# A four-layer AdaLN/FFN kernel: another order for layer 0's folded attention, filler transposes on TensorE, zeros in pieces, a bias split moved to another engine

## The chip, the cores and the metric

The kernel runs on one core of a Trainium2 chip, as one launch. The metric is the device time of one execution in microseconds; lower is better. The core has five engines that run their own instruction streams: PE (TensorE: matmuls and transposes), DVE (VectorE), ACT (ScalarE), POOL (GpSimd) and SP (SyncE, here only an issuer of transfers). Transfers (DMA) are issued by SP, ACT or POOL from their own streams and run on 16 DMA engines.

## The reference

Tokens are x of shape (32, 64, 256): 2048 tokens of 256 features in 32 sequences, and one condition vector of 256 features per sequence. All values are float32. Four layers follow one another; each is `x = x + ffn(cond(x))`, with a part that conditions the tokens and a feed-forward part:

- Layer 0: attention with 16 heads of every token against two keys, a learnt no-op key and a key made from the condition of its sequence, then a projection; then a router (softmax over 8 experts, the best two are chosen), experts of 256 to 1024 to 256 with a GELU and room for 320 tokens each, and the weighted sum of their outputs, which is added to x.
- Layer 1: a shared expert and experts that are chosen per sequence from the pooled tokens, then a mixture with entmax weights.
- Layer 2: a recurrence over the 64 positions of a sequence, with three terms of a bias, then experts again.
- Layer 3: attention and feed-forward parts with norms, and a gated feed-forward whose weights are rounded to four-bit floats.

For layer 0's attention, with two keys, the softmax of a head is a function of one difference of scores:

```python
score = q . (k_cond - k_noop)                  # per token and head
w     = exp(min(score, 0)) / (exp(min(score,0)) + exp(-max(score,0)))
out   = v_noop + w * (v_cond - v_noop)         # per head, then W_proj and b_proj
```

## The kernel before

The 2048 tokens lie as 16 tiles of 128 tokens (`NT`), in four groups of four tiles (`NG`, `GT`). PE's products go to banks of PSUM (`bank`, 512 columns; `wide`, 1024 columns). `evacuate` copies a bank to SBUF by ACT and DVE in turn: one counter, `self.turn`, decides for every call in the whole program, so that a copy that no longer goes through it changes the engine of all later ones. The instructions of each engine stand in the order in which a scheduler puts them by their priority in the program; `issue_after(mark)` places an instruction right behind another one on its engine.

*Layer 0's attention* (`fold_scores`, `fold_output`, `layer0`). Instead of making q for each token, the kernel folds Wq into the keys. PE turns `cond` (L179); DVE copies it to `condT` and ACT makes `siluT` from the same bank (L182; used in layer 1 only). PE multiplies it with `wkv` (L769); DVE subtracts the no-op key (`diff`, L772) and spreads the difference over heads (`kx` for keys, `vx` for values, L775). PE turns the four leaves of Wq, a bank of 128 by 512, which is copied to `wqT` (L110 or L112, through `evacuate`). From `kx` and `wqT` PE makes `A` (L791, 8 matmuls). The constants of the scores, bq times the keys, are `z0`: 16 recorded matmuls of one column each (L797) and one copy (L800). After that come the values' half (L769 again) and a loop over the four groups: turn X (L138, the copies to `XT` all by ACT, L141), scores `XT` times `A` (L880), and the softmax of two (DVE L885, L886, L889 to L892; ACT L887, L888). `fold_output` turns W_proj (copied to `wpT` through `evacuate`), folds the router's weights in (L830 to L840) and makes `M` (L848). A last loop makes the features that go to the experts and the router scores, `C` (L905 to L907), the softmax of the router, and the flags of the two chosen experts (L915), and SP writes `C` to a table in DRAM.

The X loads, 512 KB each, are issued by ACT (L869), as are `wq` and `wkv`, and 2176 KB of zeros for `acc_c` (L923), a buffer in DRAM into which layer 1 adds its results. All other loads of the start are SP's, in program order.

*Layer 0's experts* (`routed`, `slots`, `positions`). PE counts each expert's tokens from the flags (L318, L319); DVE computes every token's slot. For each expert a pass of 16 matmuls (L405) turns one-hot matrices made by DVE (`oh`, L363) into the lists of tokens `l0f_read` and `l0f_add`. Four passes come before the first gather; the others, 64 matmuls, lie between the two matrices of expert 0 (the "half pass" ends the first lot). POOL gathers an expert's tokens from the table with indirect transfers (L490), PE turns them (L498), then come the first matrix (L448), GELU on ACT (L450), the second matrix (L457), the bias on DVE (L514), scaling on ACT (L515) and an indirect transfer by POOL that adds the rows to `acc` in DRAM (L516). These additions run one after the other. Beside the experts DVE rounds layer 3's weights (`last_weights`). After the last expert SP reads `acc` back as X (L931).

*Layer 1 and 2.* Layer 1 turns X (L138), writes it to a table (`table_x`, issued by ACT, L946), runs the shared expert and, from sums over the tokens (`agg`, L973 to L977, and `C`, L960), the choice of experts. In the same stretch `recurrent_weights` prepares layer 2: it splits the recurrence's bias `b` into three bfloat16 terms (cast L1120, copy L1121, subtraction L1123, on DVE). Layer 2 uses `slots` and `routed` with `by_position=True`.

*Fillers.* `repeat(mark, n)` issues n transposes of a constant matrix into a bank that nobody reads, right behind `mark` on PE (L118). Before the change only layer 2 has them, 14 after the counts, 3 after each of the first four slot passes and 4 after the half pass:

```python
if by_position:
    self.repeat(self.last_count, 14)
```

Of the kernel before, what the change touches and what calls it, by code (L numbers as in the profile page):

```python
# [9 lines left out]
F32 = mybir.dt.float32  # L10
# [4 lines left out]
AF = mybir.ActivationFunctionType  # L15
ALU = mybir.AluOpType
# [4 lines left out]
P = 128  # L21
NB = 32
NS = 64
N = NB * NS
NT = N // P
D = 256
DC = D // P
FF = 1024
FC = FF // P
NE = 8  # L30
# [3 lines left out]
NG = NT // GT  # L34
# [36 lines left out]
class Kernel:  # L71
# [53 lines left out]

    def transposed(self, out, srcs):

        ps = self.bank()
        for i, s in enumerate(srcs):
            self.nc.tensor.transpose(ps[:, i * P:(i + 1) * P], s, self.ident)  # L130
        self.evacuate(out, ps[:, :len(srcs) * P].rearrange("p (n q) -> p n q", q=P))

# [24 lines left out]
    def constants(self):  # L157
        nc, cp, I = self.nc, self.cp, self.I
        self.ident = cp.tile([P, P], F32, name="ident")
        make_identity(nc, self.ident)  # L160
        self.ones_row = cp.tile([1, 512], F32, name="ones_row")
        nc.gpsimd.memset(self.ones_row, 1.0)
        iota = cp.tile([P, P], I32, name="iota_i")
        nc.gpsimd.iota(iota, pattern=[[1, P]], base=0, channel_multiplier=0)
        self.iota = cp.tile([P, P], F32, name="iota")
        nc.vector.tensor_copy(self.iota, iota)
        part = cp.tile([P, 1], I32, name="part_i")
        nc.gpsimd.iota(part, pattern=[[0, 1]], base=0, channel_multiplier=1)
        self.part = cp.tile([P, 1], F32, name="part")
        nc.vector.tensor_copy(self.part, part)  # L170


        cond = self.xp.tile([NB, D], F32, name="cond")
        nc.sync.dma_start(cond, I["cond_1024"])
        self.condT = cp.tile([P, DC, NB], F32, name="condT")
        self.siluT = cp.tile([P, DC, NB], F32, name="siluT")
        ps = self.bank()
        for c in range(DC):
            nc.tensor.transpose(ps[:, c * NB:(c + 1) * NB], cond[:, c * P:(c + 1) * P], self.ident[:NB, :NB])  # L179
        view = ps[:, :DC * NB].rearrange("p (c b) -> p c b", b=NB)  # L180
        nc.vector.tensor_copy(self.condT, view)
        nc.scalar.activation(self.siluT, view, AF.Silu)  # L182

# [183 lines left out]
    def slots(self, pool, flags, capacity, name, indices, by_position=False):  # L367
# [3 lines left out]
        nc = self.nc  # L371
# [3 lines left out]
        pos = self.positions(pool, flags, NE, "sl")  # L375
        if by_position:
            self.repeat(self.last_count, 14)
        other = pool.tile(full, F32, name="sl_other")
# [15 lines left out]
        for e0, e1 in ((0, 1), (1, NE // 2), (NE // 2, NE)):  # L394
# [6 lines left out]
            for e in range(e0, e1):  # L401
                oh = self.one_hot(ohs, e, part)
                at = (e - e0) * nchunk
                for t in range(NT):
                    self.slot_pass = nc.tensor.matmul(ps[:, at:at + nchunk], oh[:, :, t], give[:, e, t],  # L405
                                                      start=(t == 0), stop=(t == NT - 1)).ins
                if by_position and e < 4:
                    self.repeat(self.slot_pass, 3)
# [52 lines left out]
    def routed(self, table, acc, pool, flags, capacity, w1s, b1, w2s, b2s, name, by_position=False, pieces=None,  # L461
               mark=None):

# [7 lines left out]
        with tc.tile_pool(name=f"{name}_h", bufs=2) as hp, tc.tile_pool(name=f"{name}_g", bufs=2) as gp:  # L471
            chunks = [(c, min(P, capacity - c * P)) for c in range(nchunk)]

            def fetch(e):
# [6 lines left out]
                if e == 0:  # L481
                    next(slots)
                    self.half_pass, self.half_oh = self.slot_pass, self.slot_oh
                    if by_position:
                        self.repeat(self.half_pass, 4)
                elif e == 1:
                    next(slots)
# [18 lines left out]
            for e in range(NE):  # L506
                w1, w2, b2, xeT, rows_of = coming
                h = self.hidden(hp, xeT[:, :, :capacity], w1, b1[:, e * FC:(e + 1) * FC], AF.Gelu, capacity)
                for c, rows in chunks:
# [4 lines left out]
                    nc.vector.tensor_tensor(y[:rows], ps[:rows, :D], b2[:rows], ALU.add)  # L514
                    nc.scalar.activation(y[:rows], y[:rows], AF.Copy, scale=rows_of[c][:rows, D + e:D + e + 1])  # L515
                    nc.gpsimd.indirect_dma_start(  # L516
# [225 lines left out]
    def fold_scores(self, kp, loads):  # L742
# [17 lines left out]
        nc.vector.tensor_tensor(less, cols[:, 0:4], cols[:, 4:8], ALU.subtract)  # L760
        bq = cols[:, 8:10]
        diff = kp.tile([P, 4, NB], F32, name="diff")
        by_head = []
        for i, name in enumerate("kv"):
# [14 lines left out]
            if i:  # L779
                break  # L780
            wqT = kp.tile([P, DC, D], F32, name="wqT")
            self.transposed(wqT.rearrange("p m (c q) -> p (m c) q", q=P),
                            [wq[:, c, m * P:(m + 1) * P] for m in range(DC) for c in range(DC)])
            self.A = kp.tile([P, DC, NB * NH], F32, name="A")
            half = NH // DC
            for c in range(DC):
# [6 lines left out]
                self.evacuate(self.A[:, c], ps)  # L793
            ps = self.bank()
            for g in range(NG):
                for m in range(DC):
                    nc.tensor.matmul(ps[:, g:g + 1], self.of_group(x, m, g), bq[:, m:m + 1],  # L797
                                     start=(m == 0), stop=(m == DC - 1))
            self.z0 = kp.tile([P, NG], F32, name="z0")
            nc.vector.tensor_copy(self.z0, ps[:, :NG])  # L800

# [12 lines left out]
    def of_group(self, x, m, g):  # L814

        return x[:, m, g * 2 * GT:(g + 1) * 2 * GT].rearrange("p b h -> p (b h)")

    def fold_output(self, kp, loads, vx):
# [32 lines left out]
    def layer0(self):  # L851
# [11 lines left out]
        with tc.tile_pool(name="l0s", bufs=1) as sp:  # L863
            with tc.tile_pool(name="l0c", bufs=1) as kp, tc.tile_pool(name="l0t", bufs=2) as tp:
# [7 lines left out]
                for g in range(NG):  # L872
                    for t in range(g * GT, (g + 1) * GT, 2):
                        self.tile_features(XT, self.X, t, nc.scalar.copy)

                    ps = self.bank()
# [7 lines left out]
                    w = kp.tile([P, P], F32, name=f"at_w{g}")  # L884
                    nc.vector.tensor_scalar(mx, ps[:, :P], self.z0[:, g:g + 1], 0.0, ALU.add, ALU.max)  # L885
                    nc.vector.scalar_tensor_tensor(d, ps[:, :P], self.z0[:, g:g + 1], mx, ALU.add, ALU.subtract)  # L886
                    nc.scalar.activation(w, d, AF.Exp)  # L887
# [30 lines left out]
                nc.sync.dma_start(acc_rows[:, NT], self.X[:, 0])  # L918

            self.accc = self.dp.tile([N + P, D], F32, name="acc_c")  # L920
            zero = self.xp.tile([P, D], F32, name="zero")
            nc.gpsimd.memset(zero, 0.0)
            nc.scalar.dma_start(self.accc.rearrange("(t p) d -> p t d", p=P),  # L923
                                zero.unsqueeze(1).to_broadcast([P, NT + 1, D]))
            with tc.tile_pool(name="fp4w", bufs=1) as kp:
                pieces = self.last_weights(kp)
                self.routed(table, acc, sp, flags, capacity, I["L0_ffn_w1"], self.bias["L0_ffn_b1"],
                            I["L0_ffn_w2"], I["L0_ffn_b2"], "l0f", pieces=pieces)
        self.X = self.rp.tile([P, NT, D], F32, name="X", tag="X")
# [169 lines left out]
    def recurrent_weights(self, rp):  # L1099
# [19 lines left out]
        for i in range(3):  # L1119
            nc.vector.tensor_copy(cut, b)  # L1120
            nc.vector.tensor_copy(three[i * NB:i * NB + 1], cut[i * NB:i * NB + 1])  # L1121
            if i < 2:
                nc.vector.tensor_tensor(b, b, cut, ALU.subtract)  # L1123
        ones = rp.tile([K, NB], BF16, name="b_ones")
# [901 lines left out]
```

## Time and profile before

| | |
|---|---|
| median of 3 runs | 1856.86 us (1856.2, 1856.86, 1864.89) |
| the profiled execution | 1859.04 us, its span 1857.3 us |
| granted TensorE clock, mean | 0.886 |
| busy: PE, DVE, ACT, POOL | 1573.2, 711.3, 597.5, 574.3 us |
| layer 0's attention to the first slot pass | 0 to 64.08 us |
| layer 0's experts | 64 to 253.7 us |
| layer 1 from the first turn of X | 259.31 us on |

The profile follows one execution. Times are in us from the start of the span; a row of the timeline gives the start, the duration, the engine, the source line, the operation with its output and inputs, the number of instructions in the group, and in brackets how long the engine had been idle and whose work ended that. PEld is PE's load of weights, which runs beside PE. A row with the letter q behind the engine (ACTq, SPq) is the issuing of a transfer, not the transfer. The granted clock is the share of full speed that the TensorE had. A window's row gives the busy time of each engine with the number of instructions, then the clock, the busy share of the DMA engines and GB/s.

### The profile page before, as it was taken

What the parts mean: (1) busy time and instruction counts of PE and PEld (TensorE: products, weight loads), DVE (VectorE), ACT (ScalarE), POOL (GpSimd) and SP (SyncE); (2) the same over time, 40 slices, a digit from 0 to 9 for tenths busy, and PEclk for the clock granted to TensorE, in tenths of its full rate; (3) what the DMA queues carried; (4) which work ended last, traced back from release to release, by engine and by line L of the source; (5) the groups of instructions that cost most, each with busy time, mean ns of one, the idle gap of its engine ahead of it and who ended that gap; (6) DMA issues with size and microseconds to landing.
All of it is one profiled execution on the core that took longest, in us unless ns stands there. A gap on an engine that the chain in (4) does not pass through costs nothing.

```text
span 1857.3 us, 27210 instructions
## 1 busy us (share of the span) xinstructions
PE 1573.2 (85%) x10195; PEld 1216.6 (66%) x10195; DVE 711.3 (38%) x2402; ACT 597.5 (32%) x1308; POOL 574.3 (31%) x740
## 2 busy tenths in 40 slices
PE   6799997999996939999798899999655768778767
PEld 5567766888886728888676576667443546546445
DVE  3684034111111171111224510100556578786765
ACT  2222332333331203333211123222235444655443
POOL 0234311233320013332100333422235445555452
PEclk9689998999997959999888899999766779787789
DMA  7455552466632055665214154432301100101000
GB/s 267 138 148 137 133 139 67 144 203 185 201 95 88 6 162 158 202 190 160 65 29 113 37 140 120 124 94 61 95 30 35 35 18 24 35 12 32 15 12 12
DMA packets 158408, 183.84 MB, mean 99 GB/s; under 512 B 37540, under 2 KB 137536, under 8 KB 158272
## 3 DMA queue, kind: packets, MB, share of 16 engines
q1 hardware_dynamic: 123920, 143.34, 24.1%
q0 software_dynamic: 21248, 29.24, 8.9%
q10 hardware_dynamic: 13104, 9.47, 1.7%
q8 instruction: 83, 1.36, 0.3%
q14 instruction: 53, 0.43, 0.1%
HBM read 152.22 MB, written 29.79 MB: 98 GB/s over the span
## 4 chain that ended last, share of the span: by engine, by line
PE 28%; DVE 9%; POOL 6%; issue 5%; ACT 4%; DMA 2%; SPq 0%; POOLq 0%; DVEq 0%; ACTq 0%
PE bank L457 6%; PE bank L448 6%; PE bank L1172 3%; PE bank L1921 2%; PE bank L1805 2%; PE bank L1728 1%; PE bank L1502 1%; PE bank L1863 1%; DMA acc<-y,pl_add 1%; PE bank L1938 1%; ACT squares L1647 1%; PE wide L118 1%; POOL mag L1397 1%; PE bank L1839 1%; PE bank L1640 1%
## 5 line engine op out<-in xcount | busy, mean ns | idle before, releaser
L457 PE MATMUL bank<-w,hidden 128*128 128x256 f32 (+1 forms) x2080 | 472.2, 383 | 0.9 <-DVE xeT L112 0.9
L457 PEld LDWEIGHTS bank<-w,hidden 128*128 128x128 f32 (+1 forms) x2080 | 388.6, 189 | 67.5 <-issue 6.5
L448 PE MATMUL bank<-xeT,w 128*128 128x256 f32 (+2 forms) x1440 | 394.2, 432 | 2.0 <-issue 1.5
L448 PEld LDWEIGHTS bank<-xeT,w 128*128 128x128 f32 x1440 | 276.6, 193 | 109.4 <-issue 64.5
L661 DVE TENSOR_TENSOR y<-bank,b 128x256 f32<-128x256 f32 x58 | 24.6, 424 | 338.8 <-PE bank L457 333.9
L514 DVE TENSOR_TENSOR y<-bank,b 128x256 f32<-128x256 f32 (+1 forms) x56 | 23.7, 423 | 299.5 <-PE bank L457 299.5
L450 ACT ACTIVATE hidden<-bank,ge_cols 128x256 f32<-128x256 f32 x232 | 109.8, 473 | 84.8 <-PE bank L448 84.5
L450 ACT ACTIVATE hidden<-bank,bias_cols_b 128x256 f32<-128x256 f32 (+1 forms) x128 | 73.6, 580 | 108.9 <-PE bank L448 107.3
L516 POOL DMA_INDIRECT acc<-y,l2f_add x32 | 50.6, 1580 | 157.2 <-ACT xeT L110 54.5
L663 POOL DMA_INDIRECT acc_c<-y,pl_add x30 | 47.8, 1594 | 112.7 <-ACT hidden L450 80.8
L490 POOL DMA_INDIRECT xg<-table,l2f_read x32 | 35.8, 1119 | 144.4 <-ACT l2f_read L411 134.9
L663 POOL DMA_INDIRECT acc<-y,pl_add x28 | 44.5, 1591 | 105.8 <-ACT hidden L450 74.2
L516 POOL DMA_INDIRECT acc<-y,l0f_add x24 | 43.1, 1796 | 108.9 <-ACT y L515 75.0
L515 ACT ACTIVATE y<-y,xg 128x256 f32<-128x256 f32 (+1 forms) x56 | 28.5, 509 | 145.0 <-DVE y L514 139.8
L1921 PE MATMUL bank<-wg,yT 128*128 128x352 f32 x128 | 56.6, 572 | 16.7 <-ACT h_glu L1923 7.2
L1728 PE MATMUL bank<-wqkv,mo_uT 128*128 128x512 f32 (+1 forms) x128 | 56.7, 597 | 16.0 <-ACT ex L1792 13.6
L110 ACT COPY xeT<-bank 128x256 f32<-128x256 f32 (+1 forms) x57 | 20.7, 363 | 148.9 <-PE bank L130 102.6
L639 POOL DMA_INDIRECT xg<-table_x,pl_read x30 | 31.7, 1057 | 112.0 <-DVE pl_empty L592 57.6
L448 PE MATMUL bank<-XT,w 128*128 128x256 f32 x256 | 64.7, 408 | 1.7 <-DVE C L960 1.0
L1938 PE MATMUL bank<-wd,hT 128*128 128x256 f32 x192 | 60.1, 453 | 6.1 <-ACT hT L1642 2.9
L1921 PE MATMUL bank<-wu,yT 128*128 128x352 f32 x128 | 56.4, 568 | 9.9 <-DVE h_glu L1925 9.1
L662 ACT ACTIVATE y<-y,gate 128x256 f32<-128x256 f32 x58 | 29.5, 509 | 103.2 <-issue 77.0
(588 smaller groups left out, 2533.5 us busy)
## 6 DMA issues: line engine op xcount, KB each, us to landing
w<-in_L_ffn_W_dram SPq DMA_DIRECT2D x44, 1024.0 KB
w<-in_L_cond_ew_dram SPq DMA_DIRECT2D x30, 1024.0 KB
w<-in_L_ffn_w_dram SPq DMA_DIRECT2D x16, 1024.0 KB
ad<-ada SPq DMA_DIRECT2D x64, 128.0 KB
X<-acc SPq DMA_DIRECT2D x12, 512.0 KB
w<-in_L_cond_sw_dram SPq DMA_DIRECT2D x4, 1024.0 KB
ad<-ada SPq DMA_DIRECT2D x64, 64.0 KB
b<-in_L_ffn_b_dram SPq DMA_DIRECT2D x30, 128.0 KB
```

What stands on the lines that cost most here:

```text
L448: nc.tensor.matmul(ps[:, :cols], w1[:, c, f * P:(f + 1) * P], xT[:, c, :], start=(c == 0), stop=(c == DC - 1))
L450: nc.scalar.activation(h[:, f, :cols], ps[:, :cols], func, bias=bias[:, f:f + 1])
L457: self.nc.tensor.matmul(ps[:rows, :D], h[:, f, at:at + rows], w2[:, f, :], start=(f == 0), stop=(f == FC - 1))
L490: nc.gpsimd.indirect_dma_start(out=xg[:rows], out_offset=None, in_=table, in_offset=bass.IndirectOffsetOnAxis(ap=indices[e * nchunk + c][0 ...
L516: nc.gpsimd.indirect_dma_start(out=acc, out_offset=bass.IndirectOffsetOnAxis(ap=indices[e * nchunk + c][1][:rows], axis=0), in_=y[:rows], ...
L639: nc.gpsimd.indirect_dma_start(out=xg, out_offset=None, in_=table, in_offset=bass.IndirectOffsetOnAxis(ap=read[:, c:c + 1], axis=0), bound ...
L663: nc.gpsimd.indirect_dma_start(out=acc, out_offset=bass.IndirectOffsetOnAxis(ap=add[:, c:c + 1], axis=0), in_=y, in_offset=None, bounds_ch ...
L1172: last = nc.tensor.matmul(into[s // steps][q * NB:(q + 1) * NB, at:at + width], state(c), w[:, c, q].rearrange("p m f -> p (m f)"), start= ...
L1728: nc.tensor.matmul(ps[:, :hi - lo], uT[:, j, c], K["wqkv"][:, c, lo:hi], start=(c == 0), stop=(c == DC - 1))
L1805: nc.tensor.matmul(ps[rows, h * (HD + 1):(h + 1) * (HD + 1)], ex[rows, r, j * DC + c, odd], V[rows, j, h], start=True, stop=True)
L1921: nc.tensor.matmul(ps[:, :half], yT[:, c], w[:, c, cols], start=(c == 0), stop=(c == DC - 1))
L1938: nc.tensor.matmul(ps[:, :D], hT[:rows, k], self.wd[:rows, k], start=(k == 0), stop=(k == KC - 1))
```

## The change

There are six edits.

1. The copy of Wq's turned leaves is always DVE's (`nc.vector.tensor_copy`), no longer by turn; all later turns flip.
2. The constants of the scores are made per group, two matmuls and a copy (`fold_constant`) after the group's X has been turned, instead of all at once behind `A`.
3. The zeros of `acc_c` are written in seven pieces of two or three tiles, each issued by ACT behind the scaling of the first rows of experts 1 to 7.
4. Filler transposes also in layer 0: 12 after the turn of `cond`, 4 after the turn of Wq, 10 after the counts, 3 after each of the first four slot passes, 8 after the half pass.
5. `siluT` is made from `condT` in SBUF, not from the PSUM bank.
6. The split of the recurrence's bias (three casts, three copies, two subtractions) is POOL's instead of DVE's.

The order of SP's transfers is the same as before. On POOL the eight new operations stand before layer 1's first gather. On ACT, the load of the table for Exp now follows the first copies of X, and the issue of `table_x` stands after two XT copies where it stood after four; on DVE, small casts for the attention (`bits`, `ramp`) now stand before the copy of the rows `cols`. In layer 2's recurrence some matmuls that prepare it stand in another order.

```diff
-    def transposed(self, out, srcs):
+    def transposed(self, out, srcs, copy=None):
...
-        self.evacuate(out, ps[:, :len(srcs) * P].rearrange("p (n q) -> p n q", q=P))
+        (copy or self.evacuate)(out, ps[:, :len(srcs) * P].rearrange("p (n q) -> p n q", q=P))
...
+        self.unread = self.wide()
+        self.repeat(last.ins, 12)
         view = ps[:, :DC * NB].rearrange("p (c b) -> p c b", b=NB)
         nc.vector.tensor_copy(self.condT, view)
-        nc.scalar.activation(self.siluT, view, AF.Silu)
+        nc.scalar.activation(self.siluT, self.condT, AF.Silu)
...
-        if by_position:
-            self.repeat(self.last_count, 14)
+        self.repeat(self.last_count, 14 if by_position else 10)
...
-                if by_position and e < 4:
+                if e < 4:
                     self.repeat(self.slot_pass, 3)
...
-                    if by_position:
-                        self.repeat(self.half_pass, 4)
+                    self.repeat(self.half_pass, 4 if by_position else 8)
...
+                    if c == 0 and e and beside:
+                        with self.tc.issue_after(scaled.ins):
+                            beside(e)
...
-                            [wq[:, c, m * P:(m + 1) * P] for m in range(DC) for c in range(DC)])
+                            [wq[:, c, m * P:(m + 1) * P] for m in range(DC) for c in range(DC)],
+                            nc.vector.tensor_copy)
+            self.repeat(self.last_turn, 4)
...
-            ps = self.bank()
-            for g in range(NG):
-                for m in range(DC):
-                    nc.tensor.matmul(ps[:, g:g + 1], self.of_group(x, m, g), bq[:, m:m + 1],
-                                     start=(m == 0), stop=(m == DC - 1))
-            self.z0 = kp.tile([P, NG], F32, name="z0")
-            nc.vector.tensor_copy(self.z0, ps[:, :NG])
+            self.kx = x
...
+    def fold_constant(self, kp, g):
+
+        nc = self.nc
+        ps = self.bank()
+        for m in range(DC):
+            nc.tensor.matmul(ps[:, :1], self.of_group(self.kx, m, g), self.cols[:, 8 + m:9 + m],
+                             start=(m == 0), stop=(m == DC - 1))
+        z = kp.tile([P, 1], F32, name=f"z{g}")
+        nc.vector.tensor_copy(z, ps[:, :1])
+        return z
...
                         self.tile_features(XT, self.X, t, nc.scalar.copy)
+                    z = self.fold_constant(kp, g)
...
-            nc.scalar.dma_start(self.accc.rearrange("(t p) d -> p t d", p=P),
-                                zero.unsqueeze(1).to_broadcast([P, NT + 1, D]))
+            sums = self.accc.rearrange("(t p) d -> p t d", p=P)
+
+            def beside(e):
+
+                lo, hi = ((NT + 1) * k // (NE - 1) for k in (e - 1, e))
+                nc.scalar.dma_start(sums[:, lo:hi], zero.unsqueeze(1).to_broadcast([P, hi - lo, D]))
...
-            nc.vector.tensor_copy(cut, b)
-            nc.vector.tensor_copy(three[i * NB:i * NB + 1], cut[i * NB:i * NB + 1])
+            nc.gpsimd.tensor_copy(cut, b)
+            nc.gpsimd.tensor_copy(three[i * NB:i * NB + 1], cut[i * NB:i * NB + 1])
             if i < 2:
-                nc.vector.tensor_tensor(b, b, cut, ALU.subtract)
+                nc.gpsimd.tensor_tensor(b, b, cut, ALU.subtract)
```

More of the change, by code (lines that the diff above doesn't have):

```diff
@@ L124, in row_broadcast @@
         return t
-    def transposed(self, out, srcs):
+    def transposed(self, out, srcs, copy=None):
         ps = self.bank()
         for i, s in enumerate(srcs):
-            self.nc.tensor.transpose(ps[:, i * P:(i + 1) * P], s, self.ident)
-        self.evacuate(out, ps[:, :len(srcs) * P].rearrange("p (n q) -> p n q", q=P))
+            self.last_turn = self.nc.tensor.transpose(ps[:, i * P:(i + 1) * P], s, self.ident).ins
+        (copy or self.evacuate)(out, ps[:, :len(srcs) * P].rearrange("p (n q) -> p n q", q=P))
     def tile_features(self, dst, src, t, copy=None):
@@ L178, in constants @@
         for c in range(DC):
-            nc.tensor.transpose(ps[:, c * NB:(c + 1) * NB], cond[:, c * P:(c + 1) * P], self.ident[:NB, :NB])
+            last = nc.tensor.transpose(ps[:, c * NB:(c + 1) * NB], cond[:, c * P:(c + 1) * P], self.ident[:NB, :NB])
+        self.unread = self.wide()
+        self.repeat(last.ins, 12)
         view = ps[:, :DC * NB].rearrange("p (c b) -> p c b", b=NB)
         nc.vector.tensor_copy(self.condT, view)
-        nc.scalar.activation(self.siluT, view, AF.Silu)
+        nc.scalar.activation(self.siluT, self.condT, AF.Silu)
     def more_constants(self):
@@ L461, in routed @@
     def routed(self, table, acc, pool, flags, capacity, w1s, b1, w2s, b2s, name, by_position=False, pieces=None,
-               mark=None):
+               mark=None, beside=None):
         nc, tc = self.nc, self.tc
@@ L514, in routed @@
                     nc.vector.tensor_tensor(y[:rows], ps[:rows, :D], b2[:rows], ALU.add)
-                    nc.scalar.activation(y[:rows], y[:rows], AF.Copy, scale=rows_of[c][:rows, D + e:D + e + 1])
+                    scaled = nc.scalar.activation(y[:rows], y[:rows], AF.Copy,
+                                                  scale=rows_of[c][:rows, D + e:D + e + 1])
+                    if c == 0 and e and beside:
+                        with self.tc.issue_after(scaled.ins):
+                            beside(e)
                     nc.gpsimd.indirect_dma_start(
@@ L760, in fold_scores @@
         nc.vector.tensor_tensor(less, cols[:, 0:4], cols[:, 4:8], ALU.subtract)
-        bq = cols[:, 8:10]
         diff = kp.tile([P, 4, NB], F32, name="diff")
@@ L884, in layer0 @@
                     w = kp.tile([P, P], F32, name=f"at_w{g}")
-                    nc.vector.tensor_scalar(mx, ps[:, :P], self.z0[:, g:g + 1], 0.0, ALU.add, ALU.max)
-                    nc.vector.scalar_tensor_tensor(d, ps[:, :P], self.z0[:, g:g + 1], mx, ALU.add, ALU.subtract)
+                    nc.vector.tensor_scalar(mx, ps[:, :P], z, 0.0, ALU.add, ALU.max)
+                    nc.vector.scalar_tensor_tensor(d, ps[:, :P], z, mx, ALU.add, ALU.subtract)
                     nc.scalar.activation(w, d, AF.Exp)
@@ L922, in layer0 @@
             nc.gpsimd.memset(zero, 0.0)
-            nc.scalar.dma_start(self.accc.rearrange("(t p) d -> p t d", p=P),
-                                zero.unsqueeze(1).to_broadcast([P, NT + 1, D]))
+            sums = self.accc.rearrange("(t p) d -> p t d", p=P)
+            def beside(e):
+                lo, hi = ((NT + 1) * k // (NE - 1) for k in (e - 1, e))
+                nc.scalar.dma_start(sums[:, lo:hi], zero.unsqueeze(1).to_broadcast([P, hi - lo, D]))
             with tc.tile_pool(name="fp4w", bufs=1) as kp:
                 pieces = self.last_weights(kp)
+                self.unread = self.wide()
                 self.routed(table, acc, sp, flags, capacity, I["L0_ffn_w1"], self.bias["L0_ffn_b1"],
-                            I["L0_ffn_w2"], I["L0_ffn_b2"], "l0f", pieces=pieces)
+                            I["L0_ffn_w2"], I["L0_ffn_b2"], "l0f", pieces=pieces, beside=beside)
         self.X = self.rp.tile([P, NT, D], F32, name="X", tag="X")
```

## The prediction

> **What bounds the kernel now.** I read the page first, then the start in order of time, then windows of 5 us, then the places that the diff touches later on.
>
> ```profile
> PE 1573.2 (85%) x10195; PEld 1216.6 (66%) x10195; DVE 711.3 (38%) x2402; ACT 597.5 (32%) x1308; POOL 574.3 (31%) x740
> ...
> PEclk9689998999997959999888899999766779787789
> ```
>
> TensorE is the bound on average, so work off its path costs nothing, and every pause of it or half clock on it does. The second slice of its clock (46 to 93 us) is the weak one of the early part: there layer 0 routes its tokens. The start, from the timeline (start, us, engine, line, operation, and in brackets what ended the idle time):
>
> ```profile
> 1.82 10.68 ACTq L869 DMA_DIRECT2D X<-in_x_dram  x4
> ...
> 12.54 1.28 ACT L182 ACT_TABLE_LOAD   x1 [12.54 <-DMA X<-in_x_dram]
> ...
> 13.95 0.58 ACT L110 COPY wqT<-bank 128x512 f32<-128x512 f32 x1
> 14.58 3.06 PEld L791 LDWEIGHTS bank<-kx,wqT 128*128 128x128 f32 x8 [5.26 <-ACT wqT L110]
> ...
> 18.16 3.41 PE L797 MATMUL bank<-cols,kx 128*128 128x1 f32 x16
> ...
> 21.43 1.89 PE L769 MATMUL bank<-condT,wkv 128*128 128x32 f32 x8
> ...
> 23.13 1.95 PE L138 MATMUL bank<-ident,X 128*128 128x128 f32 x8
> ```
>
> ACT issues the four loads of X from its own queue and is held there until 12.5; then it loads a table, does siluT, and only then copies Wq's turned leaves, which PE had finished at 9.72. PE waits 4.9 us, then does 3.3 us of tiny matmuls for z0. No token is touched before 23.13. That stage ends where L835 can begin, behind DVE's copy of wpT:
>
> ```profile
> 38.35 0.68 DVE L112 COPY wpT<-bank 128x512 f32<-128x512 f32 x1
> ...
> 40.57 1.71 PE L835 MATMUL bank<-wpx,cols 128*128 128x264 f32 x4 [0.41 <-DVE wpx L832]
> ```
>
> From there to expert 0 one chain follows another (M, C, flags, counts, slots, gather). The windows of 5 us show PE part idle and its clock at half there (the clock is behind the POOL column, then the DMA share):
>
> ```profile
> 60.00:65.00 5.00, 2.16 (x19) 1.90 (x20) 4.06 (x16) 0.00 (x0) 0.00 (x0) 0.50 0.88 276
> ...
> 70.00:75.00 5.00, 2.66 (x8) 1.79 (x9) 1.86 (x4) 0.64 (x2) 4.09 (x4) 0.50 0.44 115
> 75.00:80.00 5.00, 5.00 (x13) 3.31 (x12) 5.00 (x10) 2.62 (x4) 0.59 (x1) 0.64 0.08 18
> ```
>
> So expert 0's first stage is longer than that of a later expert:
>
> ```profile
> 73.86 11.20 PE L448 MATMUL bank<-xeT,w 128*128 128x320 f32 x32 [0.35 <-issue]
> ```
> ```profile
> 127.30 8.88 PE L448 MATMUL bank<-xeT,w 128*128 128x320 f32 x32
> ```
>
> **The change part by part.** All sums go against the profiled execution, 1859.04 us (its span is 1857.3), which stands 2.2 above the median of 1856.86.
>
> *Wq's leaves by DVE, siluT from SBUF.* L791 then needs kx and wqT, both on DVE, and ACT's hold no longer matters. kx ended at 10.34; in the new order DVE does bits and ramp in its idle 3.0 us before 7.01, so I leave kx at about 10.2 and add 0.68 for the copy (the row of wpT, the same shape): L791 at 10.9 instead of 14.58, −3.7. ACT still copies half of A, which it can from 13.8 on, after table and siluT; PE finishes L791 only about then.
>
> *z0 out of PE's way.* L797 goes from between L791 and L769: −3.3 (18.16 to 21.43). L791 (3.6) and L769 (1.7) from 10.9 end at 16.2, so the first token is turned there instead of at 23.13, −6.9, if the clock stays at half; the twelve and four fillers, about 3 us of PE work in its pauses before, may bring the full clock by 13 or so, and then it is 14.3, −8.9. I take 15.0: −8.1. X is not late for that: three of the four issues have left ACT by 12.13. The same 8 matmuls come back as two per group ahead of its scores, with a copy of 0.16 on DVE: 4 × (2 × 0.21 + 0.16) = 2.3 at most if nothing covers it. The cover is ACT, which copies a group's four XT halves while PE idles in gaps of 0.2 to 1.3 us; I take 0.
>
> *The rest of that stage.* From 23.13 to 40.57 are 17.4 us. Until 27.2 the transposes stand 0.213 us apart, after it 0.109; some 24 matmuls gain 0.1 each if the clock comes earlier (2.4). The turn of copies by ACT and DVE flips with the first edit, so wpT goes to ACT, which is idle from 35.9, while DVE has five operations queued before it at 38.35 (0.8 more). From 0 to −3.2 together; I take −2.0. So L835 starts near 30.5, and all of the chain behind it shifts by 10.1.
>
> *Zeros of acc_c in seven pieces.* 2176 KB leave the first 40 us, where the DMA share is 1.06 to 1.09. This gains nothing: PE's waits there are for ACT, and after 40 us the share falls to 0.01. Each piece is one issue on ACT, after its first y scaling of experts 1 to 7. X's issues show what such an issue can hold ACT; its slack is 7.7 us here (scaling ends at 142.22, next GELU at 149.89). [...] The last piece runs beside the chain of acc at the end (POOL 242.93, 247.53, 252.24, each waiting 2 to 3 us for the DMA before), 0 to 1.5: +0.5.
>
> *Fillers in routing.* Ten after the counts lie in PE's wait of 2.63 us for DVE's oh (1.29 us at full clock, 2.37 at half): hidden. Three after each of four passes lengthen a pass, as layer 2 shows, where this code already runs:
>
> ```profile
> 1036.34 1.69 PE L118 MATMUL wide<-ident 128*128 128x128 f32 x14
> ...
> 1040.83 1.15 PE L405 MATMUL bank<-sl_give,oh 128*128 128x4 f16 x16
> ...
> 1042.51 1.12 PE L405 MATMUL bank<-sl_give,oh 128*128 128x4 f16 x16
> ...
> 1050.69 16.00 PE L448 MATMUL bank<-xeT,w 128*128 128x512 f32 x32 [0.56 <-issue]
> ```
>
> The period is 1.68 there and 1.45 here without them: 4 × 0.22 = +0.8 at worst. At best expert 0's L448 takes 8.88 instead of 11.20, −2.3. Layer 2 lost its clock in spite of the fillers (0.50 in 1045 to 1050; 16.00 for L448, where its later experts take 13.73), so I take a third of the gain, −0.7.
>
> *Recurrence's bias by POOL.* In layer 1 DVE does eight operations for it, late because b lands late, between those that lead to C:
>
> ```profile
> 278.29 0.29 DVE L1120 CAST b_cut<-b 96x256 bf16<-96x256 f32 x1 [6.64 <-DMA b<-in_L_cond_b_dram]
> ...
> 281.85 4.58 PE L448 MATMUL bank<-XT,w 128*128 128x256 f32 x20 [1.02 <-DVE C L960]
> ```
>
> PE's wait of 1.02 goes: −1.0 (0 to −1.5). On POOL eight operations at no more than 1.1 us (its 128x256 row) end near 288, and its next gather is at 311.73. That gather is the work queued behind, with 23 us to spare.
>
> *Orders.* The load of table_x from X stands on ACT behind two XT copies instead of four: 0 to 1, +0.5. Layer 2's recurrence gets some preparatory matmuls in another order: 0 ± 1.
>
> Sum: −8.1 − 2.0 − 0.7 − 1.0 + 0.5 + 0.5 = −10.8, so 1848.2 for an execution like the profiled one and **1846.1** against the median. The bounds alone give −16.9 to −2.6 and one more for the orders.
>
> **The rivals.** About 0.5% (9.3 us) is what a measurement of this kernel can tell from no change.
>
> (a) *Half clock throughout the start.* Stretches of tiny matmuls at 18 to 23 did not raise the clock, and one filled to some 75% (13.5 to 17.0) did not either. Then −6.9, nothing from the rest of the stage, +0.8 for the fillers, −1.0 and +1.0: −6.1, 1850.7.
>
> (b) *Fillers hold the clock into expert 0.* L448 then gains 2.3, and L457 of expert 0 (9.88 against 7.32 later, its clock 0.72 in 90 to 95 after 64 slot passes that moved little) gains 2.6 through the eight fillers behind the half pass: 4.9 in place of 0.7, −15.0, 1841.9. For it: the wait for the gather, 2.65 us, is what is left idle; against it: layer 2's row above. The Trainium skill ("TensorE: Matmul & The Clock Gate", Part 1, "What's actually happening") speaks for it: it says that a free-running window of 3.4 us kept busy lets the clock up, and an idle one brings it down. The trace agrees on the grid (changes at 27.2, 40.85, 44.27, 78.3 are multiples of 3.41 apart) and leaves open how full a window has to be. By that rule the time would be this rival's 1841.9; by layer 2's row with the whole +0.8 it would be 1847.6.
>
> (c) *Absorbed.* The chain comes 10 us early and waits at a transfer whose time is fixed: weights of expert 0, or w_q on SP, whose share of 0.88 to 0.96 in 60 to 70 is right where the gather waits. Those loads follow the table's rows on the same queue, so they come earlier too; that speaks against. Leaving 3 us of gain: 1854.
>
> (d) *Slower: the pieces hold ACT.* If each piece holds ACT as long as the four issues of X together, 10.68 us, the GELU behind it is late by 3.0, seven times: +20.9, with −10.8 it is +10.1, 1867. It loses from a hold of 9.2 on (7.7 + 10.8/7) and by 0.5% from 10.6. Against it: nothing loads DMA in these windows as at the start (share 0.45 in 125 to 145).
>
> **How the numbers follow.** Forecast 0.42 (its own range 1841 to 1852), (a) 0.18, (b) 0.17, (c) 0.13, (d) or another mishap of its size 0.10. Of the forecast 0.30 lies beyond 9.3 us of gain; with (b) and 0.03 of (a) faster has 0.50. Same: the other 0.12, 0.15 and 0.13, 0.40. Slower: 0.10. The range leaves out (d) and the low tail of (b), and reaches to (a) and (c): 1839.5 to 1856.
>
> **What would show it.** Right: L791 near 10.9 behind DVE's wqT; first X transposes at 14.3 to 16.2; L835 near 30.5 and the first slot pass near 54; no wait of PE at C of layer 1. The fillers: L448 of expert 0 between 8.9 and 11.2 and the slot passes' period, 1.45 or 1.68. Wrong: L791 waiting for another engine, a first gather that did not move by 10, or GELUs behind a piece that start late.

## The result and the profile after

The changed kernel took 1841.16 us (median of 4 runs, 1839.04 to 1847.87), the kernel before 1857.82 beside it: a ratio of 0.9911, 95% interval 0.9889 to 0.9933. Run once more with the experiments it took 1844.77 (6 runs, 1838.40 to 1850.01) against 1856.52: 0.9938 (0.9915 to 0.9960). By these ratios it gains 16.5 us in the first comparison and 11.5 in the second; the forecast was 10.8. The profiled execution of the first comparison took 1847.87 (span 1846.2), the slowest of its four.

From the page of the changed kernel, the lines that answer to those of before:

```profile
PE 1576.7 (85%) x10241; PEld 1222.2 (66%) x10241; DVE 707.3 (38%) x2397; ACT 598.8 (32%) x1308; POOL 579.0 (31%) x748
...
PEclk9699998999997959999897799999767878787789
```

The averages say nearly nothing: PE has a few more instructions (the fillers) and the second slice of its clock is what it was. What moved is seen in the timeline of the start, changed kernel (line numbers have moved: L797 was L791, L773 L769, L846 L835, L449 L448, L458 L457):

```profile
7.95 0.28 PE L761 MATMUL bank<-ident,rows 12*128 12x12 f32 x1 [1.36 <-DMA rows<-in_L_cond_b_proj_dram]
...
11.51 0.68 DVE L131 COPY wqT<-bank 128x512 f32<-128x512 f32 x1
11.96 1.28 ACT L184 ACT_TABLE_LOAD   x1 [11.96 <-DMA X<-in_x_dram]
12.25 3.06 PEld L797 LDWEIGHTS bank<-kx,wqT 128*128 128x128 f32 x8 [0.82 <-DVE wqT L131]
...
15.82 1.07 PE L773 MATMUL bank<-condT,wkv 128*128 128x32 f32 x8
...
16.73 1.07 PE L138 MATMUL bank<-ident,X 128*128 128x128 f32 x8
...
32.67 1.76 PE L846 MATMUL bank<-wpx,cols 128*128 128x264 f32 x4 [1.33 <-DVE wpx L843]
```

ACT is held until 11.96 as before, but nobody waits for it: L797 follows DVE's wqT. In this execution the rows of biases landed late: L761 and L797 start 1.3 us later than in the second profile of the same kernel (7.95 against 6.68, 12.25 against 10.98). L797 also took longer (3.78 us against 2.64), so the first tokens and the fold are 2.5 us later. The second profile shows what was forecast:

```profile
10.98 2.64 PE L797 MATMUL bank<-kx,wqT 128*128 128x256 f32 x8 [0.42 <-DVE wqT L131]
...
14.26 1.07 PE L138 MATMUL bank<-ident,X 128*128 128x128 f32 x8
...
30.20 2.13 PE L846 MATMUL bank<-wpx,cols 128*128 128x264 f32 x4 [1.33 <-DVE wpx L843]
```

The routing: windows of 5 us of the changed kernel (first profile), and expert 0:

```profile
55.00:60.00 5.00, 4.50 (x50) 4.01 (x49) 4.89 (x10) 0.26 (x1) 1.99 (x1) 0.50 0.96 294
60.00:65.00 5.00, 5.00 (x43) 4.76 (x42) 3.27 (x8) 0.27 (x1) 4.28 (x3) 0.50 0.55 136
65.00:70.00 5.00, 3.95 (x10) 2.40 (x10) 3.39 (x5) 0.37 (x1) 3.49 (x3) 0.50 0.26 71
```
```profile
67.42 10.44 PE L449 MATMUL bank<-xeT,w 128*128 128x320 f32 x32 [0.43 <-issue]
```

PE is filled to 4.50 and 5.00 of 5 us, and the clock stays at 0.50 all the same. In layer 1 the wait of 1.02 us ahead of the expert products is gone, with the bias on POOL, at 0.39 us for a cast:

```profile
269.12 0.39 POOL L1137 CAST b_cut<-b 96x256 bf16<-96x256 f32 x1 [23.71 <-DMA b<-in_L_cond_b_dram]
...
271.61 4.58 PE L449 MATMUL bank<-XT,w 128*128 128x256 f32 x20
```

### The profile page after: what moved, and what is told of

Same layout as the page of the kernel before. It is cut to its first block, busy times and chain, and to the rows that moved or that the text cites. A ratio compares the mean times of both kernels' runs of the same rounds, so it can differ in the third digit from the quotient of the medians.

```text
span 1846.2 us, 27322 instructions
## 1 busy us (share of the span) xinstructions
PE 1576.7 (85%) x10241; PEld 1222.2 (66%) x10241; DVE 707.3 (38%) x2397; ACT 598.8 (32%) x1308; POOL 579.0 (31%) x748
## 4 chain that ended last, share of the span: by engine, by line
PE 42%; DVE 11%; POOL 6%; issue 5%; ACT 3%; DMA 3%; SPq 0%; POOLq 0%; DVEq 0%; ACTq 0%
PE bank L449 13%; PE bank L458 13%; PE bank L1938 2%; PE bank L1189 2%; PE bank L1822 2%; PE bank L1745 1%; PE bank L1955 1%; PE bank L1519 1%; PE bank L1856 1%; ACT squares L1664 1%; DMA acc_c<-y,pl_add 1%; PE bank L1657 1%; PE wide L118 1%; DMA acc<-y,pl_add 1%; DVE mag L1421 1%
## 5 line engine op out<-in xcount | busy, mean ns | idle before, releaser
L458 PE MATMUL bank<-w,hidden 128*128 128x256 f32 (+1 forms) x2080 | 472.6, 383 | 0.0
L458 PEld LDWEIGHTS bank<-w,hidden 128*128 128x128 f32 (+1 forms) x2080 | 388.7, 189 | 67.4 <-issue 6.5
L449 PE MATMUL bank<-xeT,w 128*128 128x256 f32 (+2 forms) x1440 | 394.0, 432 | 1.9 <-ACT xeT L110 1.4
L449 PEld LDWEIGHTS bank<-xeT,w 128*128 128x128 f32 x1440 | 276.2, 192 | 109.3 <-issue 62.5
L666 DVE TENSOR_TENSOR y<-bank,b 128x256 f32<-128x256 f32 x58 | 24.6, 425 | 332.7 <-PE bank L458 332.7
L668 POOL DMA_INDIRECT acc<-y,pl_add x28 | 44.4, 1586 | 106.4 <-ACT hidden L451 68.8
L521 POOL DMA_INDIRECT acc<-y,l0f_add x24 | 38.9, 1622 | 105.8 <-ACT y L516 56.5
L118 PE MATMUL wide<-ident 128*128 128x128 f32 x306 | 65.2, 342 | 0.0
L449 PE MATMUL bank<-XT,w 128*128 128x256 f32 x256 | 63.8, 403 | 0.4 <-ACT hidden L451 0.4
L1938 PE MATMUL bank<-wu,yT 128*128 128x352 f32 x128 | 54.3, 549 | 10.1 <-DVE h_glu L1942 9.3
L667 ACT ACTIVATE y<-y,gate 128x256 f32<-128x256 f32 x58 | 29.5, 509 | 97.5 <-issue 69.1
```

Source lines behind the costliest of these rows:

```text
L118: self.nc.tensor.transpose(self.unread[:, :P], self.ident, self.ident)
L449: nc.tensor.matmul(ps[:, :cols], w1[:, c, f * P:(f + 1) * P], xT[:, c, :], start=(c == 0), stop=(c == DC - 1))
L458: self.nc.tensor.matmul(ps[:rows, :D], h[:, f, at:at + rows], w2[:, f, :], start=(f == 0), stop=(f == FC - 1))
L521: nc.gpsimd.indirect_dma_start(out=acc, out_offset=bass.IndirectOffsetOnAxis(ap=indices[e * nchunk + c][1][:rows], axis=0), in_=y[:rows], ...
L668: nc.gpsimd.indirect_dma_start(out=acc, out_offset=bass.IndirectOffsetOnAxis(ap=add[:, c:c + 1], axis=0), in_=y, in_offset=None, bounds_ch ...
L1938: nc.tensor.matmul(ps[:, :half], yT[:, c], w[:, c, cols], start=(c == 0), stop=(c == DC - 1))
```

## The experiments

The time differs by some microseconds from execution to execution of one kernel, so each variant is read twice: by its ratio to the kernel before on the same chip, and by distances between landmarks on PE in its profile. The landmarks, in us: *fold*, the start of L835 (L846 after); *flags*, from there to the first slot pass; *passes*, from that to expert 0's first product; *e0*, the duration of expert 0's first matrix; *e0 to e2*, between the first products of these experts; *e2 to end*, from there to the last weights turned in layer 0 (L1472); *layer 1*, from the shared expert's first product (266.14 before) to its second half's second matrix (289.54); *rest*, from there to PE's last matmul.

| kernel | ratio | fold | flags | passes | e0 | e0 to e2 | e2 to end | layer 1 | rest |
|---|---|---|---|---|---|---|---|---|---|
| before | | 40.6 | 23.5 | 9.8 | 11.2 | 53.4 | 124.8 | 23.4 | 1564.7 |
| after | 0.9911 | 32.7 | 23.5 | 11.2 | 10.4 | 52.4 | 123.1 | 22.2 | 1563.6 |
| after_again | 0.9938 | 30.2 | 24.6 | 11.1 | 11.1 | 53.2 | 123.2 | 22.2 | 1560.9 |
| turn_wq | 0.9989 | 36.1 | 24.8 | 11.0 | 8.9 | 50.7 | 124.6 | 22.3 | 1563.9 |
| z_once | 0.9935 | 32.4 | 22.5 | 10.8 | 8.9 | 51.0 | 123.3 | 22.2 | 1565.4 |
| turn_z | 0.9987 | 40.3 | 24.3 | 11.2 | 10.7 | 52.7 | 124.6 | 22.3 | 1563.5 |
| no_fill | 0.9946 | 32.6 | 23.5 | 10.4 | 11.1 | 49.9 | 123.3 | 22.2 | 1564.4 |
| no_start_fill | 0.9942 | 35.8 | 23.3 | 10.5 | 8.9 | 50.9 | 123.3 | 22.2 | 1564.9 |
| no_route_fill | 0.9936 | 31.3 | 23.5 | 9.4 | 11.3 | 50.5 | 123.4 | 22.2 | 1567.4 |
| late_fill | 0.9942 | 30.5 | 24.7 | 10.9 | 8.9 | 47.4 | 127.4 | 22.2 | 1562.2 |
| zero_once | 0.9924 | 31.4 | 23.3 | 11.2 | 10.5 | 49.6 | 123.4 | 22.2 | 1562.0 |
| split_dve | 0.9977 | 30.7 | 24.7 | 10.4 | 8.9 | 50.8 | 123.4 | 29.5 | 1560.4 |
| split_early_b | 0.9945 | 30.7 | 21.8 | 11.2 | 10.4 | 52.3 | 123.3 | 24.1 | 1564.4 |
| only_split | 0.9989 | 37.7 | 23.5 | 10.3 | 11.2 | 53.7 | 124.9 | 22.3 | 1564.4 |

One row shows how far a single profile can be read. only_split has the start of the kernel before, and its first products come at the same place (L791 at 14.57 against 14.58). Yet its 16 matmuls of one column took 1.84 us and not 3.41, and its fold is 2.9 us earlier:

```profile
18.15 1.84 PE L797 MATMUL bank<-cols,kx 128*128 128x1 f32 x16
...
37.73 1.29 PE L835 MATMUL bank<-wpx,cols 128*128 128x264 f32 x4 [0.41 <-DVE wpx L832]
```

The granted clock had risen to full at 18.1 in only_split and at 27.4 in the kernel before. So differences of *fold* below some 3 us, from one profile each, do not tell two kernels apart.

**The change once more (after_again).**

> The changed kernel once more, for a second profile and more times beside the variants. If the profiled execution of the change (1847.87 us, against 1839 to 1842 for its other executions) was slow by an accident of the throttle in layers 2 and 3, this profile ends layer 1 at the same place (about 10.8 us ahead of the kernel before at layer 1's last expert) and differs behind it; the median is 1839 to 1843. If 1847.87 was the cost of a wait that belongs to the change, the trace differs within layer 0 or 1.

1844.77 us, a little above the range. Layer 1's second half came 11.2 us ahead of the kernel before (10.2 in the first profile). Behind that point the two profiles differ by 2.7 us, and all fourteen by up to 7.0 (1560.4 to 1567.4) with no order by edit. So of the 3.7 us by which the first profile is behind, 1.0 came up to there, after the late rows, and 2.7 behind it, where the change only moves a few matmuls.

**The start: both edits undone (turn_z), each alone (turn_wq, z_once).**

```diff
# turn_wq: the copy by turn again
-                            nc.vector.tensor_copy)
+                            )
# z_once: all constants behind A, as in the kernel before; turn_z: both
-                    z = self.fold_constant(kp, g)
+                    z = self.z0[:, g:g + 1]
```

> The change with the copy of Wq's leaves by turn (so by ACT, and all later turns as before) and the constants of all groups at once behind A, as before. Fillers, pieces of zeros, siluT from SBUF and the split by POOL stay. Theory: this undoes 7.9 us of the start: 1848 to 1850, first X transposes at 21 to 23. Rival (the fillers alone bring the clock early and do most of it): 1842 to 1845, with first X transposes at 19 or earlier.

> The change with one edit undone: the copy of Wq's leaves goes by turn again (ACT), and with it all later turns are as before. Theory: L797 starts when ACT has done its table load and siluT, near 14 as before instead of 11.0, so all of layer 0 comes 2.5 to 3.5 us later; the six experts from expert 2 to the end of layer 0 take 124.8 us with the old turns instead of 123.3 (PE waits 0.9 once for the last xeT copy on DVE): together 4 to 5 us slower than the change, 1848 to 1850. Rival (the turns cost nothing and the start's clock makes up for it): 1844 to 1846 and 123.3 us.

> The change with one edit undone: the constants of all groups at once behind A. Theory: L773's second half and the first X transposes come 1.7 us (full clock) to 3.4 us (half clock) later than in the change (14.3), the stage ends 1 to 3 us later, experts 2 to 7 stay at 123.3 us: 1845 to 1848. Rival (tiny matmuls bring the clock down, so that X is turned at half clock): first X transposes near 17.5 and 0.213 us apart, the stage 4 or more later, 1849.

turn_z: 1855.94 us, 0.9987 (0.9971 to 1.0004): no gain is left that can be told. turn_wq: 1855.78, 0.9989 (0.9970 to 1.0007). Both are slower than the 1848 to 1850 that was expected. z_once: 1846.26, 0.9935 (0.9915 to 0.9955), the time of the change. So without both edits of the start the gain is gone, and by the medians the copy by DVE carries it. That edit also flips all later turns. By *fold*, one profile each, against turn_z's 40.3: the copy alone 7.9 us (z_once), z's move alone 4.2 (turn_wq), both 7.6 and 10.1. The profile of turn_wq shows the old wait at the forecast place, and the X transposes at full clock behind it:

```profile
15.00 3.72 PE L796 MATMUL bank<-kx,wqT 128*128 128x256 f32 x8 [4.44 <-ACT wqT L110]
...
19.37 1.07 PE L138 MATMUL bank<-ident,X 128*128 128x128 f32 x8
```

In z_once the 16 matmuls of one column took 1.84 us, 0.11 apart, as in only_split (3.41 in the kernel before, 0.21 apart). X came 2.5 us later than at 14.26, and at half clock, as the rival said: 1.95 for eight transposes against 1.07. The fold began at 32.4 all the same, inside what the change itself shows (30.2 and 32.7):

```profile
14.03 1.84 PE L804 MATMUL bank<-cols,kx 128*128 128x1 f32 x16
15.73 1.19 PE L773 MATMUL bank<-condT,wkv 128*128 128x32 f32 x8
16.73 1.95 PE L138 MATMUL bank<-ident,X 128*128 128x128 f32 x8
```

turn_wq and turn_z also settle something that was not in the sum. Where the turns of the copies are as before (these two, before, only_split) *e2 to end* takes 124.6 to 124.9; where they are flipped, 123.1 to 123.4 (late_fill apart). The flipped turn moves an expert's last xeT copy off DVE, and one wait goes, 0.86 of these 1.5 us, here of the kernel before; the changed kernel shows no wait of PE in that stretch (134 to 236). Where the other 0.6 went was not found:

```profile
141.20 7.32 PE L457 MATMUL bank<-w,hidden 128*128 128x256 f32 x32 [0.86 <-DVE xeT L112]
```

What is open: by its profile turn_wq ends 8 us ahead of the kernel before, by its ratio only 2. At layer 1's second half it stands 3.1 and 4.1 us behind the change's two profiles, not the 9.5 of the ratios (0.9989 against 0.9938). Its twelve runs spread from 1845.05 to 1859.97, and the profiled one took 1851.3. Four of them lie at 1859.8 to 1860.0 with a mean clock of 0.878 or 0.879; the two fastest had 0.890. The runs without a profile cannot be looked into. So how much of the gain is the copy's alone is not shown.

**The fillers (no_fill, no_start_fill, no_route_fill, late_fill).** The first leaves out all fillers of layer 0, the second the 12 and 4 of the start, the third the 10, 3 and 8 of the routing. late_fill keeps those of the start and has in the routing only 20 behind the fourth pass:

```diff
# no_fill and no_start_fill
-        self.repeat(last.ins, 12)
...
-            self.repeat(self.last_turn, 4)
# no_fill, no_route_fill and (with 20 for the last) late_fill
-        self.repeat(self.last_count, 14 if by_position else 10)
+        if by_position:
+            self.repeat(self.last_count, 14)
...
-                if e < 4:
+                if by_position and e < 4:
...
-                    self.repeat(self.half_pass, 4 if by_position else 8)
+                    if by_position:
+                        self.repeat(self.half_pass, 4)
```

> The change without any filler in layer 0 (the 12, 4, 10, 4 times 3 and 8 transposes are left out; layer 2 keeps its own). Theory of the prediction: the start gains from DVE's copy and the place of z, the fillers of the routing about nothing: 0 to 3 us slower than the change (1841 to 1844), first X transposes 0.5 to 1.2 us later and at half clock, first slot pass at about the same place. Rival (fillers hold the clock, 4.9 us in expert 0 and more at the start): 6 to 9 us slower, 1847 to 1850. A third: the fillers cost more than they bring (0.2 us a pass and 0.7 before the first transposes of gathered rows): 0 to 2 us faster.

> The change without the 12 and 4 fillers of the start; those of the routing stay. Without any filler L846 began at 32.61, with them at 30.20 and 30.68 (and at 32.67 in one where the rows landed 1.1 late). Theory: L797 runs at half clock (3.8 us instead of 2.6) and the end of the stage comes 1 to 2.4 us later: 1845.5 to 1847. Rival (the fillers of the start are hidden and bring nothing): L846 at 30.2 to 30.7 and the time of the change.

> The change without the fillers of layer 0's routing (10 after the counts, 3 after each of four slot passes, 8 after the half pass are left out); the 16 of the start stay. Three traces with these fillers had the clock at 0.50 from 52 to 64 in spite of a full PE; expert 0's first stage took 10.4, 11.1 and 8.9 us. Theory: they cost 1.3 us ahead of expert 0 and bring up the clock only by luck: 0.5 to 2.5 us faster than the change (1842 to 1844 where the change has 1844.5), from L846 to expert 0's first product 34 us instead of 34.8 to 35.7. Rival (they hold the clock): 2 to 5 us slower.

> The change with other fillers in the routing: none after the counts and between the passes, 20 in one piece behind the fourth pass (4.7 us at half clock, in the wait for the gathered rows). Theory (short runs of fillers between passes of three columns do not bring up the clock, and cost 1.3 us ahead of expert 0): from the first pass to expert 0 9.4 to 10.4 us instead of 11.2, its first stage 8.9 to 10 us instead of 10.4 to 11.1: 1 to 3 us faster than the change. Rival (the clock does not come before expert 0's own products): first stage 11.2, and the time of the run without routing fillers.

no_fill 1845.3, no_start_fill 1848.63, no_route_fill 1846.82, late_fill 1845.37; the intervals of all four overlap that of the change (0.9911 and 0.9938). Beside the second measurement, 1844.77, none costs 5 us. no_route_fill and late_fill were expected to be faster than the change and were not. The fold began at 32.6 and 35.8 without the start's fillers, and at 31.1 in the mean of the seven profiles that have them and both edits of the start (30.2 to 32.7): 1.5 and 4.7 us, from two profiles, of which the first is no more than one execution can differ from another. Those of the routing cost 1.0 us ahead of expert 0 (*passes*: mean 10.9 over the nine profiles with them, 10.0 over the four without any). They bring 1.35 in expert 0's first matrix (mean 9.85 against 11.2): 8.9 four times in nine, never without. The chance lies in when the clock rises. In the traces it changes only at steps 3.41 us apart, and where these steps fall differs from execution to execution. Between the first pass and expert 0 it rose in five of the nine profiles, each time at the end of a step in which transposes took 2.8 us or more (in zero_once it fell again one step later, and *e0* was 10.5). In the other four no step there held more than 2.7 us of them; passes filled much of the rest. That is an order in nine profiles, not a test. With 20 fillers in one piece it had risen when expert 0 began:

```profile
60.40 4.16 PE L118 MATMUL wide<-ident 128*128 128x128 f32 x20
...
66.09 8.85 PE L450 MATMUL bank<-xeT,w 128*128 128x320 f32 x32 [0.43 <-ACT xeT L110]
...
128.46 0.34 PE L500 MATMUL bank<-ident,xg 64*128 64x64 f32 x2 [2.17 <-DMA xg<-table,l0f_read]
```

but *passes* did not shorten (10.9 where 9.4 to 10.4 was expected). Its 127.4 in *e2 to end* is one wait in another place: 2.17 for a gather, the last line, falls into expert 2 here and into expert 1 in the changed kernel (1.80). Over both columns late_fill needs 174.9 us, the change 175.5 and 176.5, no_route_fill 173.9. No version was found that beats the change by more than the intervals.

**The zeros (zero_once).** One transfer at the start again, no pieces.

```diff
+            nc.scalar.dma_start(self.accc.rearrange("(t p) d -> p t d", p=P),
+                                zero.unsqueeze(1).to_broadcast([P, NT + 1, D]))
...
-                            I["L0_ffn_w2"], I["L0_ffn_b2"], "l0f", pieces=pieces, beside=beside)
+                            I["L0_ffn_w2"], I["L0_ffn_b2"], "l0f", pieces=pieces)
```

> The change with the zeros of acc_c in one transfer at the start again, instead of seven pieces beside the experts. Theory: the transfer is hidden at the start and so are the pieces: the time of the change within 1.5 us (1843 to 1846), the first X transposes at the same time. Rival: 2176 KB beside the loads of X and of the rows delay the start by what they take at 380 GB/s, 5.7 us: 1848 to 1850, with PE waiting for X.

1844.19 us, 0.9924 (0.9907 to 0.9941), X at 14.4 us: the same. The pieces hold ACT no longer than any issue, here in the timeline of the changed kernel:

```profile
133.46 0.37 ACTq L939 DMA_DIRECT2D acc_c<-zero  x1
152.96 0.37 ACTq L939 DMA_DIRECT2D acc_c<-zero  x1
```

**The split of the bias (split_dve, only_split, split_early_b).** In split_dve the eight operations go back to DVE; only_split makes this edit alone in the kernel before; split_early_b is split_dve with the loads of b issued ahead of those of Wx and Wh.

```diff
# split_dve
-            nc.gpsimd.tensor_copy(cut, b)
+            nc.vector.tensor_copy(cut, b)
...
-                nc.gpsimd.tensor_tensor(b, b, cut, ALU.subtract)
+                nc.vector.tensor_tensor(b, b, cut, ALU.subtract)
# split_early_b, besides: these lines stand ahead of the loop over Wx and Wh
+        for m in range(DC):
+            nc.sync.dma_start(b[:, :, m], src[m].partition_broadcast(K))
```

> The change with the split of the recurrence's bias back on DVE; no other instruction moves. Theory: PE's wait of 1.0 us ahead of layer 1's expert products comes back: +1.0 (0.5 to 1.5), 1842. Rival: the split also holds something in layer 2's recurrence, where the profiles differ by up to 18 us at 922 and by 12.5 at the end of it: +3 or more.

> The kernel before with one edit of the six, the split of the bias by POOL; nothing else moves. Theory of the prediction: PE's wait of 1.02 us ahead of layer 1's products goes and nothing more, 1.0 to 1.5 us faster (1855). Rival from the run with the split on DVE, which lost 5.5 us between 252 and 290: the edit is worth 5 us here too, 1851.5.

> The split of the bias on DVE, as in the run that lost 7.3 us from the shared expert's first product to its second half's end, but SP issues the loads of b ahead of Wx and Wh instead of behind. Theory (the loss was DVE standing in order behind the landing of b, with the sums over the tokens behind it): b lands some 12 us earlier, PE's wait of 4.5 us for agg goes, and the time is that of the change within 1.5 us (1843 to 1846). Rival (DVE's eight operations themselves, or the two engines' sharing, cost it): the loss stays, 1851 to 1853.

only_split: 1855.7, 0.9989 (0.9972 to 1.0006), *layer 1* 22.3 instead of 23.4: the 1.1 us of the forecast, too little for the median. split_dve: 1853.37, 0.9977 (0.9964 to 0.9990), *layer 1* 29.5 instead of 22.2. So the same edit is worth 1.1 us in the old order and 7.3 in the new. split_dve shows why:

```profile
265.93 0.29 DVE L1137 CAST b_cut<-b 96x256 bf16<-96x256 f32 x1 [11.23 <-DMA b<-in_L_cond_b_dram]
...
266.80 4.52 DVE L986 TENSOR_REDUCE part<-XT 128x64 f32<-128x1344 f32 x3
...
272.54 0.80 PE L1004 MATMUL bank<-gw,agg 128*32 128x4 f32 x12 [4.49 <-DVE agg L994]
...
274.00 9.78 PE L449 MATMUL bank<-XT,w 128*128 128x256 f32 x32 [0.44 <-DVE C L977]
```

There the scheduler put the first cast ahead of the sums over the tokens (4.5 us), where it stood behind them in the kernel before. DVE idles 11.23 us for b with the sums behind it, and PE waits 4.49 for agg. Of the other 2.8 us most is the clock, which stands at 0.50 from 274 to 278: the 32 matmuls of the second half's first matrix took 9.78 us there, where the change took 7.7. With b issued first (split_early_b) that wait is gone:

```profile
254.56 0.29 DVE L1137 CAST b_cut<-b 96x256 bf16<-96x256 f32 x1 [1.25 <-DMA b<-in_L_cond_b_dram]
...
258.00 5.84 PE L449 MATMUL bank<-XT,w 128*128 128x256 f32 x24 [1.26 <-ACT XT L110]
```

*Layer 1* takes 24.1 and the median is 1846.97 (0.9945, 0.9930 to 0.9960), just above the range: the landing of b, not DVE's operations, made most of the loss. Of the 1.9 that are left, 1.26 is the wait behind the casts, now ahead of the last XT copies. The 24 matmuls behind it took 5.84 us, some 0.5 more than their share of the 7.07 that 32 take in z_once, with the clock at 1.00 from 256 on; why is not known.

## Why the prediction was right

**The start, −8.1 and −2.0.** L797 was said for 10.9, X for 15.0, the fold for 30.5; the second profile has 10.98, 14.26 and 30.20, the first, with its late rows, 12.25, 16.73 and 32.67. The step that was counted on held: the wait of 4.86 us for ACT goes with the copy, comes back without it (4.44 in turn_wq), and without both edits no gain is left. Undoing z's move by itself shows no loss in the median, though the first token is turned 2.5 us later by its profile: the two terms of −8.1 were not as separable as the sum had them. That 30.20 is so near to 30.5 is in part luck. The −3.3 for L797 was read from an execution in which it ran at 0.21 us a matmul; in only_split, with the same start, it took 1.84 us and the fold came at 37.7. Counted from there the two profiles gain 7.5 and 5.1 us at the fold. Rival (a), half clock throughout the start, is out: eight transposes took 1.07 us, as at full clock, in both profiles of the change.

**The shift behind it.** Of 10.4 us at the fold 9.3 were left at the first pass (*flags* 24.6 against 23.5); in the first profile 7.9 of 7.9. That the chain is carried whole was right within 1.1.

**The fillers of the routing, −0.7.** Right in size by luck of two terms: +1.0 and −1.35, together −0.35. The period of a pass was 1.67, as layer 2's rows said. Rival (b) had its order wrong: the "half pass" is the fourth one, so that all eight fillers lie ahead of expert 0 (one group of 11 with the last three), not between its two matrices, and L458 behind the 64 passes took 9.6 and 9.9 us as before (9.88). The rule of the Trainium skill ("TensorE: Matmul & The Clock Gate", Part 1, "What's actually happening"), that a window of 3.4 us of PE kept busy lets the clock up, does not hold for what the profile counts as busy: from 56 to 64 the second profile has PE busy 7.95 of 8 us, passes of three columns between the fillers, and a clock of 0.50; two whole steps of 3.41 us lie in that stretch. In late_fill, with 4.16 us of transposes in one piece, the clock rose. So the first median, 1841.16, stands near this rival's 1841.9 for other reasons: in the two profiles of the change expert 0's matrices gained 0.8 and 0.3 and then 0.1 and 0.0, not 4.9.

**The bias, −1.0.** 1.2 in the profiles of the change, 1.1 alone. What the step had not seen is that the other edits change the order of DVE, and that in that order the edit guards 7.3 us of their gain (29.5 against 22.2). The sum was right because it was made for all edits at once against the trace of before; adding up edits one by one would have given the bias 1.1 or 7.3, depending on which came first.

**Tail and zeros, +1.0.** From the last turned weights to layer 1's first product took 14.2 and 13.7 us, before 14.0: nothing, not +1.0. zero_once shows the zeros to be free either way, and a piece's issue takes 0.37 us of ACT, so rival (d) (decided from 9.2 on) is out. Rival (c) would have shown in a gather that did not come earlier: the first came at 58.01 instead of 65.84.

**Not in the sum.** The flipped turns gave 1.5 us in experts 2 to 7, where 0 was put. With it the steps up to layer 1 come to −10.2 and −11.2 in the two profiles, against −10.8. The medians' 11.5 and 16.5 hold the rest: behind layer 1 one execution differs from another by up to 7 us, and no edit was found to own that. The forecast 1846.1 is 4.9 above 1841.16 and 1.3 above 1844.77.

**Slips in the sum.** None of them moves the forecast. Four passes at 0.23 more are +0.9, not +0.8. The bounds −16.9 to −2.6 already hold the 1 for layer 2's orders and leave out the 2.3 of the small matmuls of z. The stretch 13.5 to 17.0 was filled to 69% (2.42 of 3.5 us), not 75%. The clock's changes stand at 27.4, 41.0, 44.4 and 78.6 in the trace, up to 0.3 later than given; their distances are multiples of 3.41 all the same.

## What to carry to other kernels

Here the engine that issued the transfers was late for its first arithmetic (12.5 us), and whoever needed that result waited. The cure was to give one copy to an engine that issues nothing and to move small work out of PE's way; without these two edits no gain was left. Edits under a scheduler do not add: undoing one in the changed kernel asks about a new order, so read where the operation lands in the queue, and what stands behind it, before its price. When the gain is 0.7% and executions of one kernel differ by 0.6%, distances between landmarks in the profiles show what medians cannot; but one profile of each is not enough where the clock alone moves a landmark by 2.9 us.

## What was not expected of the hardware

A full PE did not raise its clock: 7.95 of 8 us busy, clock 0.50, where the matmuls are of three columns between short runs of transposes; behind 4.16 us of transposes in one piece it was 0.99 from 64 to 68 (one profile). A gather's issue on POOL took 5.6 us instead of 1.1 in each of the change's profiles while DVE was full (96.73, first profile), and 8.1 in no_fill and no_route_fill; in the kernel before it was an addition's, with 6.7 (106.05). The gather behind it came late, PE waited 1.8 us for its rows, and the next 32 matmuls took 9.01 us instead of 7.32 (in no_fill, after a wait of 1.72, they took 7.32). Why the issue is slow was not tested.
